# A gated retention layer with a feed-forward block: order of the first loads, of the statistics and of the second group's norm

## The chip, the cores and the metric

The kernel runs on one core of a Trainium2 chip. The time is the device time of one execution in microseconds (us), as the median of three runs. PE is the matrix engine (TensorE), with PEld its weight loads; DVE is VectorE, ACT ScalarE, POOL GpSimd; SP is the engine that issues nearly all DMA transfers here.

## The reference

`x` and `ctx` have 64 sequences of 128 tokens and 512 columns, all float32. Four heads have 128 columns each; the feed-forward block is 1408 wide.

```python
def xattn(x, k, v):                       # x is normalised; k = v = ctx
    Q, K, V = (einsum('bshd,hde->bshe', t, Wh) for t in (xh, kh, vh))
    scores = einsum('bshe,bthe->bhst', Q, K) / sqrt(128)
    A = maximum(abs((scores * Dn[None]).sum(axis=0)), 1.0)   # a sum over all 64 sequences
    O = einsum('hst,bthe->bshe', A, V).reshape(b, s, dim)
    Y = (O - mean(O)) / sqrt(var(O) + 1e-3) * gn_gamma + gn_beta
    return relu(x @ wg_w) * Y @ wo_w

def ffn(x):
    g = (x @ gate_w.T) * gate_s
    u = (x @ up_w.T) * up_s
    return ((silu(g) * u) @ down_w.T) * down_s

x = x + tanh(g_xattn) * xattn(layernorm(x), ctx, ctx)
x = x + tanh(g_ffn) * ffn(layernorm(x))
```

`A` needs the scores of all sequences before any output can be made, so the kernel makes two passes over x.

## The kernel before, in words

**Tiling.** The 64 sequences are 16 groups of four; a group is 512 tokens. Tokens lie on the 128 partitions when they are normalised, and columns when they are multiplied. `xnT` is the normalised group, transposed. The large products are block products of a Strassen form: seven products of half-sized blocks in place of eight, each eight matmuls of 256 columns in `product`, with sums of operands made by `combine_a` and `combine_b` (lines L236 to L245) on DVE or POOL.

**Pass 1.** For each group g, `prepare` (L401) takes the statistics of four sequences (`bn`, L166 and L167), a reciprocal deviation (`inv_std`: an addition on DVE, L161, then a power on POOL, L162), the normalised tile `xn` (L194), and a transpose on PE (L173), copied to `xnT` by ACT or DVE (L419, L417). With n = 2 for group 0 and n = 4 later, the power is taken for n sequences at once. In the same round the group before is worked on: `scores` (pq at L426, sums into a bank at L436) and `project` (seven products with the gate weights `wgc`; the sums L467 and L470 on DVE read the banks), whose result goes to memory as `w_scr`. The round also prepares a part of the weights of pass 2: loads, sums on POOL, and stores to `wo_scr`, `dn_scr` and `gu_scr`.

**Between the passes.** The scores become `attn`, and `retention(0)` makes group 0's `o`, its norm, and `y`, which multiplies the gate tile `w_t` (L578). Then follow `attended(0)` and, in between, all of `retention(1)`: values pv (L528), outputs po (L538), the norm of four sequences on DVE (L166, L194, L178), a store to `sq_scr` and loads back as `yT`, which move the blocks of the transpose, five empty steps, the scaling on ACT (L588), and the multiplications of the gate on POOL (L597).

**Pass 2.** `attended` (L602) makes seven products of the gated tile with `wo_w`, loaded one by one (L613), adds them to x on DVE and POOL (L627), takes a second layer norm and transposes. `ffn` (L726) takes the gate and up weights `gu` (L717) and the down weights `dn_w` (L723). While the ffn of group g runs, attended(g+1) and retention(g+2) run beside it.

**Order.** Each stage is a generator whose `yield`s mark steps. `interleave` takes from several generators the one that has come least far by its number of steps, so that a larger number spreads a generator's steps wider. `chain` runs generators one after another. What this order traces is a priority only: a planner places every instruction on its engine's queue by its own estimate of when inputs and buffers are there, so that work traced later can be placed earlier. On the chip each queue is then worked in its fixed order. `tc.issue_after(ins)` puts what a block traces on the engine of `ins` behind `ins` in that queue, without a wait for its end.

**Buffers.** Tiles of one tag share its buffers. Tag "x" has five buffers of two sequences; tag "wo" has three, for y (four tiles, once) and the wo_w tiles (seven for each group); tag "xn" has two. The pools `rows` and `once` are closed after pass 1, and the pools of `gu` and `dn_w` lie where they were.

Of the kernel before, what the change touches and what calls it, by code (L numbers as in the profile page):

```python
# [2 lines left out]

# [6 lines left out]
F32 = mybir.dt.float32  # L10
# [18 lines left out]
def interleave(*weighted):  # L29

    runs = [[gen, steps, 0] for gen, steps in weighted if gen is not None]
    while runs:
        run = min(runs, key=lambda r: (r[2] + 1) / r[1])
        try:
            next(run[0])
            run[2] += 1
        except StopIteration:
            runs.remove(run)
# [10 lines left out]
def flamingo_gated_layer(  # L49
# [21 lines left out]
    nc = tc.nc  # L71
    P = 128
# [5 lines left out]
    GB = 4  # L78
    NG = B // GB
    TOK = GB * S  # L80
    HT = TOK // 2
    HN = DIM // 2
    KC = NC // 2
# [10 lines left out]
    att = ctx.enter_context(tc.tile_pool(name="att", bufs=1))  # L94
# [4 lines left out]

    last_load = [None]  # L100

    def load_x(g):

        pair = []
        for q in range(2):
            t = xin.tile([P, 2, DIM], F32, tag="x", name="x_t")
            b = g * GB + 2 * q
            last_load[0] = nc.sync.dma_start(out=t, in_=x[b : b + 2].rearrange("b s d -> s b d"))
            pair.append(t)
        return pair  # L110

    def load_ctx(b):
        t = cin.tile([P, H, S], F32, tag="c", name="c_t")
        nc.sync.dma_start(out=t, in_=ctxT[b])
        return t

    x_next = [load_x(0), load_x(1)]

    ident = const.tile([P, P], F32, name="ident")
    make_identity(nc, ident)  # L120
# [27 lines left out]
    bank_b = ps_bank.tile([P, TOK], F32, name="bank_b")  # L148
# [9 lines left out]
    def inv_std(dst, var, eps, n):  # L158

        ve = stat.tile([P, n], F32, tag=f"ve{n}", name="ve")  # L160
        nc.vector.tensor_scalar_add(ve, var, eps)  # L161
        nc.gpsimd.tensor_tensor(dst, ve, mhalf[:, :n], ALU.pow)  # L162

    def bn(dst, src):
        st = stat.tile([P, 6], F32, tag="bn", name="st")
        nc.vector.bn_stats(st, src)  # L166
        nc.vector.bn_aggr(dst, st)  # L167
# [87 lines left out]
    for m, k, e in ((GA11, 0, 0), (GA12, 1, 0), (7, 0, 1), (GA22, 1, 1)):  # L255
        for s in range(2):
            e0 = e * HN + s * P
            nc.sync.dma_start(
                out=wgc[:, m, s],
                in_=wg[k * HN : (k + 1) * HN, e0 : e0 + P].rearrange("(k p) i -> p k i", p=P),  # L260
            )
    c_next = [load_ctx(b) for b in range(GB)]
    gates = const.tile([P, 2], F32, name="gates")
    nc.scalar.dma_start(out=gates[:, 0:1], in_=g_xattn.partition_broadcast(P))
# [135 lines left out]

    def prepare(g, x_t, xnT):  # L401

        n = GB if g else 2
        for j in range(GB):
            bn(mean_var[:, g * GB + j, :], x_t[j // 2][:, j % 2, :])
            if (j + 1) % n == 0:
                cols = slice(g * GB + j + 1 - n, g * GB + j + 1)
                inv_std(rstd[:, cols], mean_var[:, cols, 1], LN_EPS, n)
        yield
        for j in range(GB):  # L410
            b = g * GB + j
            xn = normalised(
                x_t[j // 2][:, j % 2, :], mean_var[:, b, 0:1], rstd[:, b : b + 1]
            )
            pt = transposed(xn, "pt")
            if j % 2:
                nc.vector.tensor_copy(xnT[:, :, j * S : (j + 1) * S], pt)  # L417
            else:
                nc.scalar.copy(xnT[:, :, j * S : (j + 1) * S], pt)  # L419
            yield  # L420
# [25 lines left out]
    def project(g, xnT):  # L446

        b11, b12, b21, b22 = as_b(xnT)
        t = once.tile([P, 4, KC, HT], F32, tag="t1", name="t1")
        combine_b(nc.vector, [t[:, i] for i in range(4)], b11, b12, b21, b22)  # L450
        w = once.tile([P, 2, 2, TOK], F32, tag="w1", name="w1")
        m5 = once.tile([P, TOK], F32, tag="m5p", name="m5p")
        bank_c = bank_c0
        product(bank_a, wgc[:, GA11], b11, True)
        nc.scalar.copy(bank_c, bank_a)
        yield
        product(bank_f, wgc[:, GS1], t[:, 0], True)
        nc.scalar.copy(m5, bank_f)
        yield
        product(bank_a, wgc[:, GA12], b21, False)  # L460
        nc.scalar.activation(w[:, 0, 0, :], bank_a, AF.Relu)
        yield
        product(bank_c, wgc[:, GS2], t[:, 1], False)
        nc.scalar.copy(bank_b, bank_c)
        yield
        product(bank_c, wgc[:, GS3], t[:, 2], False)
        nc.vector.tensor_add(w[:, 1, 1, :], bank_c, m5)  # L467
        yield
        product(bank_b, wgc[:, GS4], b22, False)
        nc.vector.tensor_add(w[:, 1, 0, :], bank_b, m5)  # L470
        nc.scalar.activation(w[:, 1], w[:, 1], AF.Relu)
        yield
        product(bank_c, wgc[:, GA22], t[:, 3], False)
        nc.scalar.activation(w[:, 0, 1, :], bank_c, AF.Relu)
        for q in range(2):
            nc.scalar.dma_start(out=w_scr[g, q], in_=w[:, q])
        yield

    pending = None
    weights = prepare_weights()  # L480
    for g in range(NG):
        x_t, c_t = x_next.pop(0), c_next
        xnT = wide.tile([P, NC, TOK], F32, tag="xT", name="xnT")
        prep = prepare(g, x_t, xnT)
        next(prep)
        if g == 1:
            gate_weights()
            constants()
        elif g > 1:
            with tc.issue_after(last_load[0].ins):  # L490
                next(weights, None)
        interleave(
            (prep, GB),
            (scores(*pending) if pending else None, 2 + GB),
            (project(pending[0], pending[2]) if pending else None, 7),
        )
        x_next.append(load_x((g + 2) % NG))
        c_next = [load_ctx((g + 1) % NG * GB + j) for j in range(GB)]
        pending = (g, c_t, xnT)
# [21 lines left out]
    def retention(g, c_t, ws):  # L521
# [38 lines left out]
        if g == 0:  # L560
            for q in range(2):
                tok = slice(q * HT, (q + 1) * HT)
                for d in range(2):
                    pt = ps_mm.tile([P, KC, HT], F32, tag="mm", name="pt")
                    for c in range(KC):
                        e = (d * KC + c) * P
                        for i in range(2):
                            nc.tensor.transpose(
                                pt[:, c, i * P : (i + 1) * P], ons[2 * q + i][:, e : e + P], ident
                            )  # L570
                    y = att.tile([P, KC, HT], F32, tag="wo", name="y", bufs=3)
                    for c in range(KC):
                        e = d * KC + c
                        nc.scalar.activation(
                            y[:, c, :], pt[:, c, :], AF.Identity,
                            scale=gamma_sb[:, e : e + 1], bias=beta_sb[:, e : e + 1],
                        )
                    (helper if d else nc.gpsimd).tensor_tensor(  # L578
                        ws[q][:, d], ws[q][:, d], y, ALU.mult
                    )  # L580
                    yield
            return
# [10 lines left out]
        for d in range(2):  # L593
            for q in range(2):
                for k in range(KC):
                    w = ws[q][:, d, k, :].rearrange("p (g i b) -> p i g b", i=NQ, b=SQ)
# [83 lines left out]
    RET_STEPS = 8 + WAIT + 2  # L680
    ATT_STEPS = 8 + GB

    def new_x1nT():
        return wide.tile([P, NQ, NC, GB, SQ], F32, tag="xT", name="x1nT")

    x_t, c_t = x_next.pop(0), c_next
    c_next = [load_ctx(GB + j) for j in range(GB)]
    ws = load_gate(0)
# [3 lines left out]
    x1nT = new_x1nT()  # L692
# [213 lines left out]
    FFN_STEPS = 1 + 7 * NJ + 3 + 17  # L906
    def chain(*gens):
        for gen in gens:
            yield from gen

    def next_retention(g):

        nonlocal c_next, ws
        c_t = c_next
        ws = load_gate(g)
        yield from retention(g, c_t, ws)
        if g + 1 < NG:
            c_next = [load_ctx((g + 1) * GB + j) for j in range(GB)]

    interleave((attended(0, x_t, ws, x1nT), ATT_STEPS), (next_retention(1), RET_STEPS + 4))  # L920
    pending = (0, x_t, x1nT, combine_tokens(nc.vector, x1nT))
    for g in range(NG - 1):
        x_t = x_next.pop(0)
        x1nT = new_x1nT()
        if g + 2 < NG:
            x_next.append(load_x(g + 2))
        steps = [attended(g + 1, x_t, ws, x1nT)]
        if g + 2 < NG:
            steps.append(next_retention(g + 2))
        interleave(  # L930
            (ffn(*pending), FFN_STEPS), (chain(*steps), int((ATT_STEPS + RET_STEPS) * 1.05)),
        )
        pending = (g + 1, x_t, x1nT, combine_tokens(nc.gpsimd, x1nT))
    interleave((ffn(*pending), 1))
# [58 lines left out]
```

## Time and profile before

| | |
|---|---|
| Median of three runs | 2315.32 us (2315.17 to 2315.83) |
| Profiled execution | 2315.39 us, span 2313.6 us |
| PE busy | 2272.9 us |
| DVE, POOL, ACT busy | 851.7, 686.0, 575.6 us |
| DMA | 459.17 MB, mean 198 GB/s |
| Mean granted PE clock | 0.995 |

The span is the time from the first to the last instruction. A line of the timeline has start, duration, engine, source line, operation, output and inputs with shapes, and the number of instructions merged; in brackets stands how long the engine was idle before it, and what ended that idle time. A line of the waits has the waiting engine and its instruction, what it waited for, the sum in us, the number of waits and the longest one. A transfer's issue is an instruction of SP's queue, marked SPq.

### The profile page before, as it was taken

How to read it: one execution, taken by the hardware profiler on the slowest of the kernel's cores; microseconds unless marked ns; L12 is line 12 of the kernel's file. 1: busy time of each engine (PE TensorE's matmuls, PEld its weight loads, DVE VectorE, ACT ScalarE, POOL GpSimd, SP SyncE). 2: the span in 40 equal slices, each digit the busy share in tenths (PEclk: the TensorE clock that was granted, in tenths of full speed). 3: DMA queues.
4: the chain of work that ended last, by engine and by line, in shares of the span. 5: the costliest groups of instructions: out<-in, count | busy, mean ns of one | idle time of the engine just before them, and what ended most of it. 6: DMA issues, size and time to landing. Idle time of an engine off the chain costs nothing.

```text
span 2313.6 us, 28056 instructions
## 1 busy us (share of the span) xinstructions
PE 2272.9 (98%) x10808; PEld 1950.1 (84%) x10808; DVE 851.7 (37%) x1753; ACT 575.6 (25%) x1052; POOL 686.0 (30%) x825
## 2 busy tenths in 40 slices
PE   8999997899999999999999999999999999999999
PEld 6778786788888888888888888888888888888888
DVE  6544534433323333433333434343333333333222
ACT  2333332221213131212121222222212222222221
POOL 4232201423232424242424233232324232323210
PEclk9999999899999999999999999999999999999999
DMA  7767646456666666656565656575747565645541
GB/s 263 249 230 255 237 165 221 142 194 208 198 218 198 211 194 207 210 183 215 189 228 179 219 180 209 178 234 162 240 157 240 174 229 172 227 153 185 176 148 64
DMA packets 158181, 459.17 MB, mean 198 GB/s; under 512 B 16736, under 2 KB 36832, under 8 KB 143328
## 3 DMA queue, kind: packets, MB, share of 16 engines
q1 hardware_dynamic: 152624, 440.34, 58.2%
q10 hardware_dynamic: 5424, 17.04, 1.8%
q8 instruction: 85, 1.39, 0.2%
q14 instruction: 48, 0.39, 0.1%
HBM read 376.72 MB, written 80.61 MB: 198 GB/s over the span
## 4 chain that ended last, share of the span: by engine, by line
PE 66%; DVE 0%; issue 0%
PE bank_c L202 15%; PE bank_a L202 10%; PE bank_c L792 7%; PE bank_b L202 5%; PE bank_f L792 5%; PE bank_f L202 5%; PE by L616 3%; PE bank_b L792 2%; PE bank_a L792 2%; PE bz L616 2%; PE bx L616 2%; PE pv L528 2%; PE po L538 2%; PE bank_c L806 1%; PE bank_a L806 1%; PE bank_c L849 1%
## 5 line engine op out<-in xcount | busy, mean ns | idle before, releaser
L202 PE MATMUL bank_c<-tcomb,gu 128*128 128x256 f32 x1920 | 456.6, 379 | 0.0
L202 PEld LDWEIGHTS bank_c<-tcomb,gu 128*128 128x128 f32 x1920 | 361.3, 190 | 47.7 <-ACT bank_b L760 0.4
L202 PE MATMUL bank_a<-x1nT,gu 128*128 128x256 f32 x1280 | 302.8, 379 | 0.7 <-ACT x1nT L671 0.7
L202 PEld LDWEIGHTS bank_a<-x1nT,gu 128*128 128x128 f32 x1280 | 242.0, 190 | 33.2 <-ACT x1nT L671 0.9
L242 POOL TENSOR_TENSOR hs<-h,h 128x256 f32<-128x256 f32 x80 | 58.2, 727 | 605.1 <-DVE h L740 591.5
L162 POOL TENSOR_TENSOR rs<-ve,mhalf 128x1 f32<-128x1 f32 x128 | 72.7, 577 | 480.1 <-DVE ve L161 463.8
L739 ACT ACTIVATE sil<-c,gs_sb 128x256 f32<-128x256 f32 x160 | 81.3, 508 | 319.4 <-DVE c L769 184.5
L597 POOL TENSOR_TENSOR w_t<-w_t,yT 128x256 f32<-128x256 f32 x120 | 83.5, 728 | 259.6 <-ACT yT L588 259.6
L202 PE MATMUL bank_b<-x1nT,gu 128*128 128x256 f32 x640 | 151.2, 379 | 0.0
L202 PE MATMUL bank_f<-tcomb,gu 128*128 128x256 f32 x640 | 151.2, 379 | 0.0
L769 DVE TENSOR_TENSOR c<-bank_c,m 128x512 f32<-128x512 f32 x80 | 55.1, 688 | 246.6 <-PE bank_c L202 246.6
L792 PE MATMUL bank_c<-dn_w,hs 128*128 128x256 f32 x640 | 145.0, 382 | 0.0
L792 PE MATMUL bank_f<-dn_w,h 128*128 128x256 f32 x640 | 143.4, 379 | 0.0
L792 PEld LDWEIGHTS bank_f<-dn_w,h 128*128 128x128 f32 x640 | 121.6, 190 | 22.5 <-issue 6.7
L202 PEld LDWEIGHTS bank_b<-x1nT,gu 128*128 128x128 f32 x640 | 121.6, 190 | 22.5 <-issue 6.7
L792 PEld LDWEIGHTS bank_c<-dn_w,hs 128*128 128x128 f32 x640 | 120.3, 190 | 19.8 <-ACT bank_b L869 4.0
L202 PEld LDWEIGHTS bank_f<-tcomb,gu 128*128 128x128 f32 x640 | 121.6, 190 | 16.6
L740 DVE SCALAR_TENSOR_TENSOR h<-bank_a,us_sb,sil 128x256 f32<-128x256 f32 x80 | 38.6, 482 | 246.5 <-ACT sil L739 246.5
L166 DVE BATCH_NORM_STATS2 st<-x_t 128x6 f32<-128x512 f32 x128 | 83.0, 683 | 96.1 <-DMA x_t<-in_x_dram 95.0
L752 ACT COPY bank_c<-bank_a 128x512 f32<-128x512 f32 x80 | 45.6, 570 | 253.9 <-PE bank_a L202 253.9
L740 DVE SCALAR_TENSOR_TENSOR h<-c,us_sb,sil 128x256 f32<-128x256 f32 x160 | 77.3, 483 | 77.0 <-ACT sil L739 77.0
L760 ACT COPY bank_b<-bank_c 128x512 f32<-128x512 f32 x80 | 45.6, 570 | 203.0 <-PE bank_c L202 114.9
(165 smaller groups left out, 3575.2 us busy)
## 6 DMA issues: line engine op xcount, KB each, us to landing
gu<-gu_scr SPq DMA_DIRECT2D x80, 1024.0 KB, 4.9
dn_w<-dn_scr SPq DMA_DIRECT2D x112, 640.0 KB, 5.5
gu<-gu_scr SPq DMA_DIRECT2D x80, 768.0 KB, 6.0
x_t<-in_x_dram SPq DMA_DIRECT2D x64, 512.0 KB, 4.4
c_t<-in_ctxT_dram SPq DMA_DIRECT2D x128, 256.0 KB, 4.2
sq_scr<-sq SPq DMA_DIRECT2D x30, 1024.0 KB, 4.8
wo_w<-wo_scr SPq DMA_DIRECT2D x112, 256.0 KB, 3.9
w_scr<-w ACTq DMA_DIRECT2D x32, 512.0 KB, 5.8
```

Source lines behind the costliest of these rows:

```text
L162: nc.gpsimd.tensor_tensor(dst, ve, mhalf[:, :n], ALU.pow)
L166: nc.vector.bn_stats(st, src)
L202: nc.tensor.matmul(out, lhsT=w[:, s, k, :], rhs=x_k, start=(start and s == 0 and k == 0), stop=(s == 1 and k == KC - 1), skip_group_check= ...
L242: engine.tensor_tensor(s[0], a21, a22, ALU.add)
L528: nc.tensor.matmul(pv[:, h, :], lhsT=c_t[j][:, h, :], rhs=wh_sb[:, h, :], start=True, stop=True,)
L538: nc.tensor.matmul(po, lhsT=attn[:, h, :], rhs=v[:, h, :, :], start=True, stop=True)
L597: (helper if d else nc.gpsimd).tensor_tensor(w, w, yT[:, :, d * KC + k, q * 2 : q * 2 + 2, :], ALU.mult)
L616: nc.tensor.matmul(bank[:, i * HN : (i + 1) * HN], lhsT=lhs[:, k, i * P : (i + 1) * P], rhs=w[:, k, :], start=(start and i == 0 and k == 0 ...
L739: nc.scalar.activation(sil, src[:, 0:n], AF.Silu, scale=gs_sb[:, i : i + 1])
L740: nc.vector.scalar_tensor_tensor(dst, src[:, n : 2 * n], us_sb[:, i : i + 1], sil, ALU.mult, ALU.mult)
L769: nc.vector.tensor_add(c22, bank_c, m5)
L792: nc.tensor.matmul(bank[:, i * HN : (i + 1) * HN], lhsT=lhs[:, j, i * P : (i + 1) * P], rhs=dn[:, j, :], start=(start and i == 0 and j == ...
```

## The change

There are four parts.

- `load_x` gets an argument: the first group is loaded in four transfers of one sequence each, not in two of two. Group 1's load is traced behind the eight loads of `wgc`. In `prepare`, n is 1 for group 0.
- In pass 1 the statistics of a group are traced under `tc.issue_after` of `last_add`, the sum L470 of the last projection traced. That is project(g-2) for group g; the first two groups have none.
- `y` takes its buffers from tag "xn", two of them, in place of tag "wo".
- Only the first seven steps of next_retention(1), the values and three of the four outputs, run beside attended(0), spread by the number 10 in place of 19. What is left of it (the fourth output, the norm, the store and loads, the multiplications) runs at the head of the chain beside the first ffn; attended(1) and retention(2) follow. That chain counts 35 steps in place of 27.

```diff
@@ -1,5 +1,6 @@
 from contextlib import ExitStack
 from functools import partial
+from itertools import islice
 
 import concourse.bass as bass
 import concourse.tile as tile
@@ -99,13 +100,17 @@
 
     last_load = [None]
 
-    def load_x(g):
+    def load_x(g, at_once=2):
 
         pair = []
         for q in range(2):
             t = xin.tile([P, 2, DIM], F32, tag="x", name="x_t")
             b = g * GB + 2 * q
-            last_load[0] = nc.sync.dma_start(out=t, in_=x[b : b + 2].rearrange("b s d -> s b d"))
+            for i in range(0, 2, at_once):
+                last_load[0] = nc.sync.dma_start(
+                    out=t[:, i : i + at_once],
+                    in_=x[b + i : b + i + at_once].rearrange("b s d -> s b d"),
+                )
             pair.append(t)
         return pair
 
@@ -114,7 +119,7 @@
         nc.sync.dma_start(out=t, in_=ctxT[b])
         return t
 
-    x_next = [load_x(0), load_x(1)]
+    x_next = [load_x(0, 1)]
 
     ident = const.tile([P, P], F32, name="ident")
     make_identity(nc, ident)
@@ -259,6 +264,7 @@
                 out=wgc[:, m, s],
                 in_=wg[k * HN : (k + 1) * HN, e0 : e0 + P].rearrange("(k p) i -> p k i", p=P),
             )
+    x_next.append(load_x(1))
     c_next = [load_ctx(b) for b in range(GB)]
     gates = const.tile([P, 2], F32, name="gates")
     nc.scalar.dma_start(out=gates[:, 0:1], in_=g_xattn.partition_broadcast(P))
@@ -400,7 +406,7 @@
 
     def prepare(g, x_t, xnT):
 
-        n = GB if g else 2
+        n = GB if g else 1
         for j in range(GB):
             bn(mean_var[:, g * GB + j, :], x_t[j // 2][:, j % 2, :])
             if (j + 1) % n == 0:
@@ -467,7 +473,7 @@
         nc.vector.tensor_add(w[:, 1, 1, :], bank_c, m5)
         yield
         product(bank_b, wgc[:, GS4], b22, False)
-        nc.vector.tensor_add(w[:, 1, 0, :], bank_b, m5)
+        last_add[0] = nc.vector.tensor_add(w[:, 1, 0, :], bank_b, m5)
         nc.scalar.activation(w[:, 1], w[:, 1], AF.Relu)
         yield
         product(bank_c, wgc[:, GA22], t[:, 3], False)
@@ -476,13 +482,18 @@
             nc.scalar.dma_start(out=w_scr[g, q], in_=w[:, q])
         yield
 
+    last_add = [None]
     pending = None
     weights = prepare_weights()
     for g in range(NG):
         x_t, c_t = x_next.pop(0), c_next
         xnT = wide.tile([P, NC, TOK], F32, tag="xT", name="xnT")
         prep = prepare(g, x_t, xnT)
-        next(prep)
+        if last_add[0] is None:
+            next(prep)
+        else:
+            with tc.issue_after(last_add[0].ins):
+                next(prep)
         if g == 1:
             gate_weights()
             constants()
@@ -568,7 +579,7 @@
                             nc.tensor.transpose(
                                 pt[:, c, i * P : (i + 1) * P], ons[2 * q + i][:, e : e + P], ident
                             )
-                    y = att.tile([P, KC, HT], F32, tag="wo", name="y", bufs=3)
+                    y = att.tile([P, KC, HT], F32, tag="xn", name="y", bufs=2)
                     for c in range(KC):
                         e = d * KC + c
                         nc.scalar.activation(
@@ -917,18 +928,27 @@
         if g + 1 < NG:
             c_next = [load_ctx((g + 1) * GB + j) for j in range(GB)]
 
-    interleave((attended(0, x_t, ws, x1nT), ATT_STEPS), (next_retention(1), RET_STEPS + 4))
+    def late_attended(g, x_t, x1nT):
+        yield from attended(g, x_t, ws, x1nT)
+
+
+    second = next_retention(1)
+    interleave((attended(0, x_t, ws, x1nT), ATT_STEPS), (islice(second, 7), 10))
     pending = (0, x_t, x1nT, combine_tokens(nc.vector, x1nT))
     for g in range(NG - 1):
         x_t = x_next.pop(0)
         x1nT = new_x1nT()
         if g + 2 < NG:
             x_next.append(load_x(g + 2))
-        steps = [attended(g + 1, x_t, ws, x1nT)]
+        steps = [attended(g + 1, x_t, ws, x1nT)] if g else [second]
+        n_steps = ATT_STEPS + RET_STEPS
+        if g == 0:
+            steps.append(late_attended(1, x_t, x1nT))
+            n_steps += RET_STEPS - 7
         if g + 2 < NG:
             steps.append(next_retention(g + 2))
         interleave(
-            (ffn(*pending), FFN_STEPS), (chain(*steps), int((ATT_STEPS + RET_STEPS) * 1.05)),
+            (ffn(*pending), FFN_STEPS), (chain(*steps), int(n_steps * 1.05)),
         )
         pending = (g + 1, x_t, x1nT, combine_tokens(nc.gpsimd, x1nT))
     interleave((ffn(*pending), 1))
```

## The prediction

> **What bounds the kernel now.** I read the page first, for the busiest engine and its idle time:
>
> ```profile
> span 2313.6 us, 28056 instructions
> PE 2272.9 (98%) x10808; PEld 1950.1 (84%) x10808; DVE 851.7 (37%) x1753; ACT 575.6 (25%) x1052; POOL 686.0 (30%) x825
> ```
>
> TensorE is the bound: only 2313.6 - 2272.9 = 40.7 us of the span are without a matmul. A change that adds or removes no matmul, as this one, can gain those 40.7 us and what is lost to a lowered clock, no more. So the second view is busy time by stage:
>
> ```profile
> 0.00:20.00 20.00, 9.84 (x48) 8.20 (x48) 12.35 (x27) 3.23 (x5) 7.94 (x14) 1.00 0.89 281
> ...
> 400.00:410.00 10.00, 4.75 (x14) 3.04 (x13) 9.10 (x26) 0.00 (x0) 2.82 (x5) 0.71 0.60 215
> 430.00:440.00 10.00, 4.42 (x18) 3.04 (x17) 0.48 (x1) 2.99 (x6) 9.69 (x13) 0.91 0.53 190
> ```
>
> The columns are the stretch, its length, busy PE, PEld, DVE, ACT, POOL, clock, DMA share, GB/s. PE idles 10.2 us in the first 20; in the same view 7.2 more lie in 20 to 360 (part of it missing records), 19.4 in 360 to 450, and 3.1 in the tail. From 450 to 2000 the engine is full. All parts of the diff lie in the idle places. Third, who ended PE's waits:
>
> ```profile
> PE pq L426 <- DVE xnT L417: 8.0, 5, 2.9
> PE bx L616 <- DMA wo_w<-wo_scr: 5.7, 1, 5.7
> PE by L616 <- DVE x_t L627: 5.2, 1, 5.2
> PE bz L616 <- POOL ys L242: 3.7, 1, 3.7
> PE bx L616 <- POOL w_t L597: 1.9, 2, 1.7
> PE bank_c L202 <- DVE w L467: 1.6, 1, 1.6
> ```
>
> Fourth, the timeline around each, to see what the releaser itself stood behind:
>
> ```profile
> 18.11 1.48 DVE L194 TENSOR_SCALAR xn<-x_t,mean_var,rstd 128x512 f32<-128x512 f32 x1 [1.13 <-POOL rstd L162]
> ...
> 20.34 1.96 PE L426 MATMUL pq<-xnT,gram 128*128 128x512 f32 x4 [2.88 <-DVE xnT L417]
> ```
> ```profile
> 169.17 1.29 DVE L166 BATCH_NORM_STATS2 st<-x_t 128x6 f32<-128x512 f32 x2 [5.81 <-DMA x_t<-in_x_dram]
> ...
> 170.59 0.66 DVE L470 TENSOR_TENSOR w<-bank_b,m5p 128x512 f32<-128x512 f32 x1
> 171.17 0.68 DVE L417 COPY xnT<-pt 128x512 f32<-128x512 f32 x1
> ...
> 172.00 3.65 PE L426 MATMUL pq<-xnT,gram 128*128 128x512 f32 x4 [2.03 <-DVE xnT L417]
> ```
> ```profile
> 384.20 3.39 PE L616 MATMUL bx<-wo_w,w_t 128*128 128x256 f32 x8 [5.70 <-DMA wo_w<-wo_scr]
> ```
> ```profile
> 403.40 1.30 DVE L178 STREAM_TRANSPOSE sq<-xn 128x512 f32<-128x512 f32 x2
> ...
> 405.31 0.68 DVE L627 TENSOR_TENSOR x_t<-x_t,by 128x512 f32<-128x512 f32 x1
> ...
> 406.05 3.78 PE L616 MATMUL by<-wo_w,w_t 128*128 128x256 f32 x8 [5.17 <-DVE x_t L627]
> ```
> ```profile
> 439.37 3.78 PE L616 MATMUL bz<-wo_w,ys 128*128 128x256 f32 x8 [3.66 <-POOL ys L242]
> ```
> ```profile
> SPq L717 <- DMA w_scr<-w: 19.8, 2, 18.0
> ...
> SPq L613 <- DVE w_t L578: 0.3, 1, 0.3
> ```
>
> See in each a queue worked in its order: a statistic that waits for a load, or a norm of the next group, stands ahead of the instruction that PE needs.
>
> **The change part by part.** The sum is made against the profiled execution, 2315.39 us, its span of 2313.6 and 1.8 around it; the median of the runs, 2315.32, is the same within 0.1.
>
> *The clock, for all parts.* After the waits the matmuls run at half speed: eight of 256 columns take 3.78 us at 406.05 and at 439.37, and 1.89 elsewhere; the four of pq take 3.65 after a wait of 2.03 us, and 1.96 elsewhere. [...]
>
> *A. First x group batch by batch.* SP issues four loads of 256 KB for group 0 in place of two of 512, then passes the eight weight loads (wgc) ahead of group 1's two loads. SP's count ahead of wgc is unchanged (four x loads), 1 MB of x comes off the rings ahead of wgc, and at the 281 GB/s of this stretch that is up to 3.7 us; the other way, group 1 lands up to 3.7 later than its 11.3. [...] The page's rows weigh it: 256 KB of c_t land in a median 4.2 us, 512 KB of x_t in 4.4. By these rows the first batch is here only 0.2 us sooner; the earlier wgc and the order count for more. Added: two small DVE additions (0.15 each) and two POOL powers (0.55 to 0.9 each) as n is 1, off the path. What ends the start now is the copy of the last xnT of group 0 at 19.52, behind group 1's xn on DVE, which waits for a power that stands behind wgc's sums on POOL. Group 0's last batch lands at 7.9; bn 0.7, aggregate and addition 0.3, power 0.6, xn 0.55, transposes 0.6, copy 0.7 make 11.4. The dense stretch could so begin up to 8 us before 20.3; POOL's sums of wgc (four at 1.3 behind its landing) and the later group 1 take part of it. Bounds 8 to -1 (group 1's statistics now late); taken 4.5.
>
> *B. Statistics pinned.* Today a statistic is run more than two groups ahead, at the moment when its load lands; the row at 169.17 belongs to group 10 while group 7 is prepared. Pinned, group g's comes after the sum L470 of project(g-2), when its load is long there. The waits go: pq in pass 1 (8.0 less the 2.9 at the start, so 5.0), L467's 1.6, and half clock twice (two stretches show 0.91 over 20 us), 1.7 each: 10.0. What is late next: on DVE behind the pin stand four statistics (0.68 each), aggregates and addition 0.5, then POOL's power up to 1.2 and xn 0.54, together 5.0; in the trace the transposes of the next group come, with the wait taken out, 6.7 us after L470's product (165.2 to 171.9). The cover is GA22's product, the next bank_a and two pq. It has under 2 us to spare, less where the DVE subtractions L239 (2.7 for four) or POOL's weight sums (four at 1.27, ending at 170.2) stand in between. Bounds 10 to a loss (the slow rival); taken 8: some 2 us lost over all rounds.
>
> *C. The y tag and the norm moved out of attended(0).* y leaves "wo" for the two buffers of "xn"; four y share two slots. The third then waits for the POOL product that ends at 174.4, before its own turn: nothing. With "wo" unused until attended, the first three wo_w loads need nothing but wo_scr. The planner lets such loads run far ahead (w_scr's first two, used after 370, are issued at 48.9), so they will no longer stand behind gu, for which SP waited 18.0 us. Gain: 5.7 and 1.5 of clock (3.39 for eight). The four norms of group 1 (statistics, xn, transposes: 2 us each on DVE from 398 to 405) leave DVE ahead of the adds L627: 5.2 and 2.4 of clock (3.78 for 1.89, 1.12 for 0.63). Together 14.8. Late next: the fourth to seventh wo_w, on rings that carry 3.5 MB of gu and 0.75 of c_t from 376.7 (385 GB/s in 380 to 390: 11 us, to about 388). The products before the fourth are 5.7 us and the pv and po fill some 7, so the fourth is wanted at about 388. Bounds 14.8 to 4; taken 10.5.
>
> *D. Norm and gate of group 1 in the first FFN.* The last po, four norms, one sq_scr store and four yT loads, the ACT scaling, eight POOL products, then attended(1): all spread over FFN products, one of 36 steps at about 3.8 us, instead of attended(1) asking at once for a w_t whose yT has just come. Five empty steps, about 19 us, cover store and loads (4.8 and 5.5 by the page), three the POOL products. Today's waits: 1.9 and 3.7, and clock 3.0 (3.78 and 2.97 for two products of 1.89): 8.6. Later FFNs work in this pattern, with PE full. Bounds 8.6 to 0; taken 7.
>
> *E. What it adds.* No matmul, no bytes. The first FFN carries 35 side steps for 27; DVE gets 8 us of norms in about 137, where it is a third busy. Priced by the later FFNs at nothing, from above by one burst of norms standing ahead of a bank's sum, as at 400, 5 us with clock: taken -2.
>
> Sum: 4.5 + 8 + 10.5 + 7 - 2 = 28; 2315.4 - 28 = 2287.4.
>
> **The rivals.** *The waits move.* wo_w's wait goes to the fourth product, since SP and the rings are full of gu (for: DMA share of 1.02 in 380 to 390); the start gains nothing since group 1 is late; the first FFN's burst costs its 5. Then B 7, C 5, D 5, A 0, E -3: 14, so 2301. Against: the planner has pv and po to put in.
>
> *Slower: the pinned statistics become the path.* Place: the 14 rounds of pass 1 from group 2 on. If the power stands in POOL's queue behind the weight sums (which themselves wait for loads, 35.5 us in five waits), xn and the transposes come late and PE waits in each round. At 2 us and 1.7 of clock it is 14 x 3.7 = 52, against 30 of other gains (A 4.5, B's old waits 10, C to E 15.5): +22, 2337. It decides from 30 / 14 = 2.1 us per round, clock included. Against: 6.7 us of cover for 5.0 of chain, and PE has other products to run first.
>
> *It doesn't do what it says.* The planner issues what is ready by its own costs; the norms, ready once po is there, may slip ahead of the adds on DVE again. With B short too, that is 2313.
>
> **How the numbers follow.** My forecast has 0.62 (2277 to 2298), the moved waits 0.24, the slow rival 0.10, no effect 0.04. A measurement of this kernel can tell about 0.2% (4.6 us) from no change. Faster 0.86, same 0.04, slower 0.10. The range, 2275 to 2306, takes in forecast and moved waits, and A at 8 with B, C and D near their tops below; it leaves out the slow rival and no effect.
>
> **What would show it.** A: the first dense PE stretch begins near 16, not 20.3. B: no DVE statistic in pass 1 ends on an x load, and pq's wait on L417 is near 1 us in all. C: the first wo_w loads are issued far before 370, and the 5.7 and 5.2 are gone. D: no wait on L597 or L242 in the first FFN. PEclk is 1.00 from 100 to 500. Idle PE in total: near 20 us. It is wrong if transposes L173 wait for L194 in each round of pass 1, or if bank_c or bank_b in the first FFN waits for DVE.

## The result, and the profile after

The changed kernel takes 2333.99 us (median of six runs), the kernel before, in the runs beside it, 2316.67. The ratio is 1.0078 (1.0065 to 1.0091): slower by 17.3 us, where 28 less were forecast.

The page of the changed kernel:

```profile
span 2332.2 us, 28091 instructions
PE 2278.6 (98%) x10808; PEld 1955.0 (84%) x10808; DVE 857.9 (37%) x1755; ACT 577.2 (25%) x1052; POOL 691.2 (30%) x827
```

As many matmuls as before, and 53.6 us without one (2332.2 - 2278.6) in place of 40.7. The matmuls' busy time grew by 5.7 us too: some of them ran slower. PE's waits of the changed kernel (line numbers have moved: L178 is the transpose, L199 xn):

```profile
PE pt L178 <- DVE xn L199: 32.6, 17, 4.9
PE bz L627 <- POOL ys L247: 7.1, 2, 3.9
```

The first line stood at 2.4 us before:

```profile
PE pt L173 <- DVE xn L194: 2.4, 3, 1.1
```

Gone are the waits of pq on the copy L417, of bx on wo_w, and of by on the adds. Busy time by stage, of the changed kernel (stretch, length, busy PE, PEld, DVE, ACT, POOL, clock, DMA share, GB/s):

```profile
0.00:20.00 20.00, 13.29 (x60) 10.87 (x61) 13.38 (x31) 4.40 (x7) 9.15 (x16) 1.00 0.87 286
100.00:200.00 100.00, 88.84 (x443) 71.92 (x443) 44.44 (x84) 29.88 (x48) 29.07 (x27) 0.93 0.64 211
```

The start is better by 3.4 us of busy PE. Pass 1, nearly full before, has holes and a clock of 0.93. Three times read from the traces place it: from the first GS1 product to the last score, pass 1 went from 329.7 to 361.5 us; from there to the first ffn's GS1 product, 65.2 to 50.4; from there to the fourth store of a result, 252.1 to 258.7.

The timeline of one long round of the changed kernel:

```profile
124.59 0.69 DVE L476 TENSOR_TENSOR w<-bank_b,m5p 128x512 f32<-128x512 f32 x1 [2.31 <-PE bank_b L207]
...
127.80 1.27 POOL L249 TENSOR_TENSOR gu_raw<-gu_raw 128x512 f32<-128x512 f32 x1 [18.60 <-DMA gu_raw<-in_upT_dram]
...
129.03 1.72 POOL L247 TENSOR_TENSOR gu_raw<-gu_raw 128x512 f32<-128x512 f32 x1
...
129.63 1.67 DVE L244 TENSOR_TENSOR t<-xnT 128x512 f32<-128x512 f32 x1
...
130.82 1.59 POOL L248 TENSOR_TENSOR gu_raw<-gu_raw 128x512 f32<-128x512 f32 x1
...
131.22 1.22 DVE L166 TENSOR_SCALAR ve<-mean_var 128x4 f32<-128x4 f32 x1
...
132.49 1.66 POOL L250 TENSOR_TENSOR gu_raw<-gu_raw 128x512 f32<-128x512 f32 x1
...
134.12 1.01 POOL L167 TENSOR_TENSOR rstd<-ve,mhalf 128x4 f32<-128x4 f32 x1
135.17 0.55 DVE L199 TENSOR_SCALAR xn<-x_t,mean_var,rstd 128x512 f32<-128x512 f32 x1 [2.13 <-POOL rstd L167]
...
135.86 1.08 PE L178 MATMUL pt<-ident,xn 128*128 128x128 f32 x4 [4.80 <-DVE xn L199]
...
136.74 3.62 PE L207 MATMUL bank_f<-t,wgc 128*128 128x256 f32 x8
```

L476 is the sum that carries the pin (L470 of the kernel before). The statistics follow it, then two subtractions (L244), the addition `ve`, the power, xn and the transpose. PE waits 4.80 us, and the next product then takes 3.62 for 1.89. A short round, with no sums of gu_raw beside it:

```profile
152.84 0.69 DVE L476 TENSOR_TENSOR w<-bank_b,m5p 128x512 f32<-128x512 f32 x1 [2.31 <-PE bank_b L207]
...
153.45 0.68 DVE L423 COPY xnT<-pt 128x512 f32<-128x512 f32 x1
...
154.04 1.28 DVE L171 BATCH_NORM_STATS2 st<-x_t 128x6 f32<-128x512 f32 x2
...
156.64 0.66 DVE L244 TENSOR_TENSOR t<-xnT 128x512 f32<-128x512 f32 x1
...
157.31 0.66 DVE L244 TENSOR_TENSOR t<-xnT 128x512 f32<-128x512 f32 x1
...
157.88 0.16 DVE L166 TENSOR_SCALAR ve<-mean_var 128x4 f32<-128x4 f32 x1
...
158.12 1.38 POOL L167 TENSOR_TENSOR rstd<-ve,mhalf 128x4 f32<-128x4 f32 x1 [7.21 <-DVE ve L166]
...
159.53 0.55 DVE L199 TENSOR_SCALAR xn<-x_t,mean_var,rstd 128x512 f32<-128x512 f32 x1 [0.90 <-POOL rstd L167]
...
160.23 0.63 PE L178 MATMUL pt<-ident,xn 128*128 128x128 f32 x4 [0.93 <-DVE xn L199]
```

From the start of L476 to the transpose are 7.4 us here and 11.3 in the long round; without the wait 6.5 in both. Nine rounds wait 0.9 us, five 3.4 to 4.9.

What makes a round long has two parts. The addition `ve` ends 7.85 us behind the pin in the long round and 5.20 in the short one: the two subtractions and `ve` itself run slower while POOL works its sums (1.23 and 1.67 us for 0.66, 1.22 for 0.16). That is 2.65 us. The power then stands in POOL's queue behind the sum L250 and starts 1.7 us after `ve` has ended. In the first of the five rounds the sums come earlier, and the power starts as soon as `ve` has ended:

```profile
84.45 1.22 DVE L166 TENSOR_SCALAR ve<-mean_var 128x4 f32<-128x4 f32 x1
...
85.75 1.39 POOL L167 TENSOR_TENSOR rstd<-ve,mhalf 128x4 f32<-128x4 f32 x1
...
87.87 0.63 PE L178 MATMUL pt<-ident,xn 128*128 128x128 f32 x4 [3.43 <-DVE xn L199]
88.34 1.89 PE L207 MATMUL bank_f<-t,wgc 128*128 128x256 f32 x8
```

There the slower DVE alone makes the wait of 3.43 us, and no half clock follows it.

### The profile page after: what moved, and what is told of

The parts are those of the page before. It is cut to its first block, busy times and chain, and to the rows that moved or that the text cites. A ratio compares the mean times of both kernels' runs of the same rounds, so it can differ in the third digit from the quotient of the medians.

```text
span 2332.2 us, 28091 instructions
## 1 busy us (share of the span) xinstructions
PE 2278.6 (98%) x10808; PEld 1955.0 (84%) x10808; DVE 857.9 (37%) x1755; ACT 577.2 (25%) x1052; POOL 691.2 (30%) x827
## 3 DMA queue, kind: packets, MB, share of 16 engines
q8 instruction: 85, 1.39, 0.2%
## 4 chain that ended last, share of the span: by engine, by line
PE 92%; DVE 3%; POOL 3%; DMA 1%; issue 1%; ACT 0%; SPq 0%; POOLq 0%; ACTq 0%; DVEq 0%
PE bank_c L207 20%; PE bank_a L207 13%; PE bank_c L803 9%; PE bank_f L207 7%; PE bank_b L207 7%; PE bank_f L803 6%; PE by L627 3%; PE bank_b L803 3%; PE bank_a L803 3%; PE bz L627 3%; PE pv L539 2%; PE po L549 2%; PE bx L627 2%; PE bank_c L442 2%; PE bank_c L817 2%; PE pq L432 1%
## 5 line engine op out<-in xcount | busy, mean ns | idle before, releaser
L247 POOL TENSOR_TENSOR hs<-h,h 128x256 f32<-128x256 f32 x80 | 58.0, 726 | 582.4 <-DVE h L751 582.4
L207 PE MATMUL bank_c<-t,wgc 128*128 128x256 f32 x384 | 92.4, 383 | 0.0
```

Source lines behind the costliest of these rows:

```text
L207: nc.tensor.matmul(out, lhsT=w[:, s, k, :], rhs=x_k, start=(start and s == 0 and k == 0), stop=(s == 1 and k == KC - 1), skip_group_check= ...
L247: engine.tensor_tensor(s[0], a21, a22, ALU.add)
```

## Experiments

Each kernel was timed beside the kernel before; the ratios are to that, with their 95% intervals.

### Taking the pin out of the changed kernel

```diff
-        if last_add[0] is None:
-            next(prep)
-        else:
-            with tc.issue_after(last_add[0].ins):
-                next(prep)
+        next(prep)
```

> The changed kernel without its pin: the statistics of pass 1 are free again, the other three parts stay. Theory (the pinned statistics put the power on POOL, behind the weight sums, on PE's path; in the trace after, pass 1 from its first GS1 product to its last score takes 361.5 us, before 329.7): the transposes' waits on xn fall from 32.6 us to about 3, pass 1 loses its 31.8 us, so about 2302 and faster than before by some 14. Rival (the new order of the first loads delays the weight loads and sums of all later rounds): the pin is innocent, the time stays at 2334.

Measured: 2300.79 us, before 2316.81; ratio 0.9922 (0.9905 to 0.9939). PE's waits of this kernel:

```profile
PE bz L623 <- POOL ys L247: 7.1, 2, 3.9
PE pq L432 <- DVE xnT L423: 5.3, 3, 3.5
...
PE pt L178 <- DVE xn L199: 2.1, 3, 1.0
```

The transposes' 32.6 us are gone and the old wait of pq on the copy is back. The theory holds, the rival falls: without the pin, the other three parts are a gain of 16.0 us (2316.81 - 2300.79).

### The pin alone, in the kernel before

The same lines added to the kernel before, with `last_add` set at the sum L470.

> The kernel before with the pin alone. Theory: the same waits of about 0.9 and 4.6 us in turn, round by round, and half clock after the long ones: 2316.7 + 31.8, about 2348. Rival (the pin hurts only together with the later load of group 1 or the two buffers of xn that y takes): within 5 us of 2317.

Measured: 2351.64 us, before 2316.81; ratio 1.0138 (1.0123 to 1.0153). PE's waits on xn are those of the changed kernel:

```profile
PE pt L173 <- DVE xn L194: 33.7, 17, 5.6
```

The pin alone costs 34.8 us and needs no other part for it: the theory holds (2348 expected), the rival falls.

### The pin one round earlier

`last_add` is a list here, to which each projection appends its sum L470.

```diff
-        if last_add[0] is None:
+        if len(last_add) < 2:
             next(prep)
         else:
-            with tc.issue_after(last_add[0].ins):
+            with tc.issue_after(last_add[-2].ins):
                 next(prep)
```

> The changed kernel with the statistics of group g pinned one round earlier, behind the sum of project(g-3). Theory (what matters is how much time lies between the statistics and the transposes, some 6.7 us with the pin as it is; one round is 22 us more, and the loads have landed by then): no statistic waits for a load and no transpose for xn; pass 1 falls below that of before, by up to the 10 us that the old waits cost: 2302 less some 8, about 2294. Rival (any pin costs, since it takes the statistics out of DVE's idle time and puts them in front of the subtractions): about half of the waits stay, 2318.

Measured: 2292.95 us, before 2316.81; ratio 0.9887 (0.9871 to 0.9904). Busy time from 20 to 340 us, first of this kernel, then of the one before, then of the changed one:

```profile
20.00:340.00 320.00, 320.00 (x1722) 265.25 (x1720) 156.56 (x311) 112.13 (x182) 81.11 (x74) 1.00 0.71 239
```
```profile
20.00:340.00 320.00, 312.99 (x1648) 256.56 (x1649) 151.00 (x306) 108.08 (x177) 80.67 (x74) 0.99 0.68 230
```
```profile
20.00:340.00 320.00, 289.74 (x1489) 235.67 (x1488) 145.72 (x281) 100.33 (x161) 83.25 (x73) 0.96 0.66 219
```

From 20 us on pass 1 has no hole left, and the theory's number (2294) was met. The idea behind the pin is right: it takes away the waits of the kernel before, worth another 7.8 us beside the kernel without a pin (2300.79 - 2292.95). Only its place was wrong. Ahead of the stretch shown, at 17.21, pq waits 2.75 us where it waited 0.29 in the changed kernel: a statistic of group 1, whose load has not landed, stands on DVE ahead of the copy that pq needs.

### The weight sums behind the power

```diff
-            with tc.issue_after(last_load[0].ins):
+            with tc.issue_after(last_load[0].ins), tc.issue_after(last_pow[0].ins):
                 next(weights, None)
```

`last_pow` holds the power that `inv_std` issued last.

> The changed kernel with the weight sums of a round pinned behind that round's power in POOL's queue. Theory (POOL's queue makes the long waits: in five rounds four sums of 1.3 to 1.7 us stand ahead of the power): the five waits of 3.4 to 4.9 fall to about 0.9 as in the other rounds, 18 us less, and the half clock after them, some 10: 2334 less 28, about 2306. Rival (DVE's own chain is late: four statistics, subtractions and the addition come too late whatever POOL does): the long waits shrink by less than 2 us each, 2322 or more.

Measured: 2318.28 us, before 2316.81; ratio 1.0001 (0.9991 to 1.0011). That is 15.7 us less than the changed kernel, between the two answers. PE's waits of this kernel, its busy time from 20 to 340 us, and one of its rounds:

```profile
PE pt L179 <- DVE xn L200: 26.1, 16, 1.9
```
```profile
20.00:340.00 320.00, 295.07 (x1567) 241.18 (x1566) 178.41 (x299) 104.90 (x168) 90.47 (x74) 1.00 0.68 228
```
```profile
130.62 1.39 POOL L168 TENSOR_TENSOR rstd<-ve,mhalf 128x4 f32<-128x4 f32 x1 [15.88 <-DVE ve L167]
131.99 2.67 POOL L344 TENSOR_TENSOR dn_raw<-dn_raw,ds 128x512 f32<-128x512 f32 x2
132.05 1.49 DVE L200 TENSOR_SCALAR xn<-x_t,mean_var,rstd 128x512 f32<-128x512 f32 x1 [0.91 <-POOL rstd L168]
...
133.68 0.63 PE L179 MATMUL pt<-ident,xn 128*128 128x128 f32 x4 [1.88 <-DVE xn L200]
```

POOL was idle when the power was wanted, and no long wait is left, so POOL's sums ahead of the power did make those, with their half clock. This run moves the sums out of the way of the power and of DVE at once, so it does not tell the two parts apart; the rows of the long rounds do. Nearly all rounds now wait 1.9 us: the sums that follow the power run beside xn, which takes 1.49 for 0.55. That the short waits would stay at 0.9 was wrong, and so the total. The other 0.9 is DVE's own chain, which does not fit under the cover even with POOL free.

### The pin one product earlier

```diff
-        nc.vector.tensor_add(w[:, 1, 1, :], bank_c, m5)
+        last_add[0] = nc.vector.tensor_add(w[:, 1, 1, :], bank_c, m5)
...
-        last_add[0] = nc.vector.tensor_add(w[:, 1, 0, :], bank_b, m5)
+        nc.vector.tensor_add(w[:, 1, 0, :], bank_b, m5)
```

> The changed kernel with the pin on the sum L467 of the same projection, in place of L470: one product earlier, some 3 us in the trace after (121.59 to 124.59). Theory (the loss is lead time: the chain from the pin to xn is longer than the work of PE that covers it, by 0.9 us in the short rounds and about 4.6 in the long ones): three more us make the nine short waits vanish (8.4 us) and shorten the five long ones by 3 each (15), too short then for half clock (10): 2334 less 33, about 2301. Rival (the queue on POOL decides, where the power keeps its place behind the sums however early the statistics are): the five long waits stay whole with their half clock, only the short ones go, 2325.

Measured: 2293.92 us, before 2316.99; ratio 0.9905 (0.9889 to 0.9922). One long round of this kernel:

```profile
115.45 1.28 POOL L249 TENSOR_TENSOR gu_raw<-gu_raw 128x512 f32<-128x512 f32 x1 [17.10 <-DMA gu_raw<-in_upT_dram]
...
116.57 0.67 DVE L476 TENSOR_TENSOR w<-bank_b,m5p 128x512 f32<-128x512 f32 x1
...
120.63 1.02 POOL L167 TENSOR_TENSOR rstd<-ve,mhalf 128x4 f32<-128x4 f32 x1
...
122.76 0.60 PE L178 MATMUL pt<-ident,xn 128*128 128x128 f32 x4
```

The statistics now stand ahead of L476 and the subtractions behind xn. From group 2 on no transpose waits for xn; all that is left there are three waits of 0.3 us for a subtraction. The gain beside the changed kernel, 40.1 us, is more than the 33 worked out, since the long waits went whole. The power still comes last behind the sums, but these begin at 115.5, a microsecond ahead of L476, where they began at 127.8, three behind it, and no subtraction runs beside them: `ve` takes 0.17 us. The theory had the direction right and the size too small; the rival's queue is there, but the lead covers it. What made the weights' loads come sooner within the round was not tested; the x load that SP issues behind the late xn (136.80 in the changed kernel) stands ahead of later weight transfers in SP's queue, which would do it.

### The first loads alone

The kernel before with `load_x(0, 1)`, group 1's load behind `wgc`, and n of 1.

> The kernel before with the new order and size of the first loads alone (x batch by batch, group 1 behind wgc, n of 1). Theory: the first GS1 product comes at 18.8 in place of 22.6 us, as in the changed kernel, and all that follows is shifted by these 3.8: about 2313. Rival (the wait is only put off to group 1, whose loads are later): nothing is left at the end of the second round, 2317.

Measured: 2309.94 us, before 2316.06; ratio 0.9973 (0.9964 to 0.9983): 6.1 us less, 2 more than expected. Busy time of the first 20 us of this kernel:

```profile
0.00:20.00 20.00, 13.85 (x62) 11.23 (x62) 12.79 (x32) 4.41 (x8) 9.91 (x16) 1.00 0.88 293
```

4.0 us more of matmul than before in the same stretch. Its first GS1 product is at 18.1, before at 22.6. The rival falls. The size of the loads, their order and n were changed together here; which of them pays was not tested. The first sum of wgc starts 3.3 us sooner (10.94 for 14.27), the first statistic 0.8 (4.04 for 4.87), which speaks for the order.

### y in tag xn alone

```diff
-                    y = att.tile([P, KC, HT], F32, tag="wo", name="y", bufs=3)
+                    y = att.tile([P, KC, HT], F32, tag="xn", name="y", bufs=2)
```

> The kernel before with y in tag xn alone. Theory: the first three wo_w loads run ahead of pass 1's end, and the first product of attended(0) no longer waits 5.7 us, nor runs at half clock for 1.5: about 2309.5. Rival (the wait moves to the fourth wo_w, behind gu on the rings): within 3 us of 2317.

Measured: 2306.91 us, before 2316.06; ratio 0.9957 (0.9944 to 0.9969): 9.1 us less. PE's timeline of this kernel:

```profile
377.64 1.89 PE L616 MATMUL bx<-wo_w,w_t 128*128 128x256 f32 x8
...
397.98 3.78 PE L616 MATMUL by<-wo_w,w_t 128*128 128x256 f32 x8 [3.86 <-DVE x_t L627]
```

The first product starts 6.6 us sooner than before (384.20), at full speed and with no wait. The wait on DVE's adds stays, as the norm is still ahead of them, but is 1.3 us shorter. The theory holds, with 2.6 us more than it asked for; the rival falls.

### The norm of group 1 moved alone

The new `islice` and the chain of the changed kernel, in the kernel before.

> The kernel before with only the norm of group 1 moved to the first ffn. Theory: attended(0) loses the wait of 5.2 us and 2.4 of half clock, but the first ffn and the second keep a wait on POOL each (3.2 and 3.9 us in the changed kernel, and clock), where before had one: from the end of the scores to the 4th store of a result the changed kernel gained 8.2 in all, 7.2 of which y accounts for, so 1 remains: about 2316. Rival (the two parts need each other; without y's move the wait on wo_w grows as there is less to fill it): 2320 or more.

Measured: 2313.56 us, before 2316.06; ratio 0.9991 (0.9982 to 0.9999): 2.5 us less. PE's waits of this kernel:

```profile
PE bz L617 <- POOL ys L243: 7.1, 2, 3.8
PE bx L617 <- DMA wo_w<-wo_scr: 6.9, 1, 6.9
```

The 5.2 us on DVE's adds are gone; the waits on POOL grew from 3.7 to 7.1, and that on wo_w from 5.7 to 6.9. The rival had this last one right in kind, as fewer pv are put ahead of it, but not in size: the part is a small gain alone, near the theory's 2316.

### DVE for half of POOL's line in groups 1 and 2

On the pin one round earlier, in `retention` and in `attended`:

```diff
-        helper = nc.vector if g == 0 else nc.gpsimd
+        helper = nc.vector if g <= 2 else nc.gpsimd
```

> The kernel with the pin one round back, and DVE in place of POOL for half of the gate's multiplications and the four sums of attended in groups 1 and 2. Theory (POOL works eight multiplications and four sums in one line ahead of the second product bz, in the first and the second ffn, 3.2 and 3.9 us of wait and half clock after them): both waits go, 2293 less 7.1 and some 4 of clock, about 2282. Rival (yT comes too late, so the wait stays whoever multiplies): one of the two waits stays, 2288 or more.

Measured: 2281.25 us, before 2316.06; ratio 0.9848 (0.9835 to 0.9862). Its page:

```profile
span 2280.0 us, 28060 instructions
PE 2261.2 (99%) x10808; PEld 1947.5 (85%) x10808; DVE 863.3 (38%) x1771; ACT 575.9 (25%) x1052; POOL 674.8 (30%) x811
```

Of 7.1 us of bz's wait, 1.7 are left on DVE and 0.6 on a load. The theory holds, the rival falls. The whole kernel has 18.8 us without a matmul. This is the best version found: 34.8 us below the kernel before.

### The first ffn's side work taken faster

On the pin one round earlier, POOL keeping its work:

```diff
-            n_steps += RET_STEPS - 7
+            n_steps += RET_STEPS - 7 + 7
...
     def late_attended(g, x_t, x1nT):
+        yield
         yield from attended(g, x_t, ws, x1nT)
```

> The kernel with the pin one round back, and with the side work of the first ffn taken faster: a weight of 44 for its steps in place of 36, and one more empty step ahead of attended(1). POOL keeps its work. Theory (bz waits for POOL since product and multiplications are traced too close, in the first ffn, and since retention(2) ends too late, in the second): both waits of 3.2 and 3.9 and their clock go, about 2283. Rival (POOL's line of twelve operations is too slow wherever it is put, only DVE's help takes the waits away): 2290 or more.

Measured: 2284.62 us, before 2316.99; ratio 0.9862 (0.9847 to 0.9877), so 8.3 less than its base of 2292.95. Its waits:

```profile
PE bz L628 <- POOL ys L247: 3.2, 1, 3.2
```

The second ffn's wait of 3.9 went: POOL keeps its line of twelve there, but begins it at 506.1, 14 us ahead of the first product, where the changed kernel began it at 563.4, 0.8 us ahead. So that wait came from retention(2) ending late. The first ffn's stayed: there the empty step did not separate the multiplications from the product that needs them. Neither answer was wholly right.

## Why the prediction was wrong

The parts add up. Each alone, against the kernel before: loads -6.1, y -9.1, norm -2.5, pin +34.8: +17.1, and the whole change measured +17.3. Each of the four is known to some 2 to 4 us, so that part of this closeness is luck. Of the 45 us between forecast and result, the pin makes 43 (8 gained forecast, 34.8 lost).

**B is the step that failed**, by sign: the term "some 2 us lost over all rounds", from 5.0 us of chain (what must run on DVE and POOL between the pin and the transpose) against 6.7 of cover (PE's own work in that time). The cover was right (6.5). The chain in a short round is 7.4. What the working counted (statistics, addition, power, xn) takes 5.0 in the rows above too; what it left out is L470's own time (0.6), the copy behind it (0.6) and two of the four subtractions (1.2), which it named as a risk and did not add. That makes nine waits of 0.9. In the five long rounds POOL's sums slow the subtractions and the addition by 2.3 to 2.7 us, in all five, and hold up the power for another 1.7 in four. The prediction had named the sums too, but only as what stands ahead of the power, with 1.27 each. Its second reason against the slow rival, that PE has other products to run first, did not come true either: PE stands idle at the transpose.

The slow rival had 0.10. Its place was right, and so was its mechanism in part: the power stands behind the sums in four rounds of fourteen. That its 52 us and its 2337 came near the measured numbers is partly luck. Between the kernel pinned one round earlier and the changed one, pass 1 lost 43.0 us (361.5 in place of 318.5), but unevenly, where the rival took 3.7 for every round. The prediction's own sign of being wrong, transposes that wait for xn in each round, is the line of 32.6 us.

**The gain that B named was right.** With the pin one round or even one product earlier, the old waits go, and all that takes their place are the waits named there: one at the start with the first, three of 0.3 us with the second.

**A** was near: 4.5 taken, 6.1 measured; the dense start came at 16.55. As size and order of the loads were not run apart, nothing here speaks for or against the smaller loads.

**C** was right in its mechanism. In the changed kernel's trace SP issues the first wo_w loads far ahead:

```profile
78.47 0.34 SPq L624 DMA_DIRECT2D wo_w<-wo_scr  x1
...
79.75 0.89 SPq L624 DMA_DIRECT2D wo_w<-wo_scr  x2
```

Neither the first product nor the fourth has a long wait for a load. From the last score to the first ffn's GS1 product 14.8 us were saved. (The 174.4 in its working is 374.4 in the trace; the argument is the same.)

**D** failed too, with less weight. The prediction took 7 for it, on the sight of later ffns where this pattern costs nothing. There the gate's multiplications end ahead of attended (in the third ffn of the changed kernel at 687.0, 1.9 us ahead of its first product); in the first ffn the first product (463.97) and the sums are wanted while POOL still multiplies (462.03 to 469.0). bz waits for POOL in the first ffn and again in the second, since the longer chain ends late:

```profile
571.82 3.78 PE L627 MATMUL bz<-wo_w,ys 128*128 128x256 f32 x8 [3.85 <-POOL ys L247]
```

From the first ffn's GS1 product to the fourth store the change lost 6.6 us. C, D and E, for which 15.5 were taken, are 11.6 by the two kernels with one part each. **E** as such, the side work in the first ffn, shows in waits of 0.3 us for DVE and 0.7 for ACT only.

**The clock.** The prediction counted half speed after waits of 2 us, by one row. The runs draw no sharp limit. Waits of up to 1.9 us, with the sums behind the power, left the clock at 1.00 from 20 to 340. In the changed kernel four waits of 4.5 to 4.9 us were followed by half speed (the next eight matmuls took 3.62 us three times and 2.82 once, for 1.89; the granted clock from 186 to 190 was 0.50), and so was one of 3.22 ahead of bz (2.56 us for 1.89, then four matmuls in 1.91 for 1.03), but the one of 3.43 shown above was not. In the kernel before, two of 2.0 were (the four matmuls of pq took 3.65 and 3.22 us, for 1.88). What else decides was not tested.

## What to carry to other kernels

A pin that stops an early instruction from blocking its queue also sets the earliest time of all that hangs on it; sum the whole chain in queue order, on every engine that it crosses, before placing it. Add the rows that lie in between, not only those that the argument is about: here 2.4 us of them were enough. Give the pin the slack that is there: one product earlier turned 17 us lost into 23 gained. When stalls come from one engine's queue, look at what is ready early and runs long on the other engine (POOL's sums): here it held up what stood behind it (the power, 1.7 us in four rounds), and slowed what ran beside it (the subtractions and `ve`, 2.3 to 2.7 us in five).

## What was not expected of the hardware

DVE and POOL slow each other in some pairs of instructions. In the long round a subtraction takes 1.67 us for 0.66 and POOL's sum 1.72 for 1.27. The addition `ve`, which reads one tile of 128x4, takes 1.22 for 0.16. The power takes 1.39 beside a subtraction and 1.02 without, and xn takes 1.49 for 0.55 beside POOL's multiplication. POOL's sums stayed at 1.27 beside DVE's statistics (the one at 127.80 in that round). The sum L247 ends at 130.75, and the subtraction beside it, begun at 129.63, ends 0.55 later. How the one slows the other is not shown by this. For its chain the prediction took xn at 0.54, from rows where POOL was idle; its own row at 18.11, an xn of 1.48 us beside a sum of wgc on POOL, had shown the effect.
